# Layer 1's keys and queries by seven half-size products, in a hybrid attention kernel

## The chip, the cores and the metric

The kernel runs on one core of one Trainium2 chip. The metric is the device time of the whole program in microseconds; the runs of the kernel before took 3247.21, 3250.87 and 3253.22 us, and their median is 3250.87 us.

## The reference, cut to what matters

Four residual layers on `x` of shape (4, 1024, 256), all in fp32: attention "a", a feed-forward layer (256 to 1024 to 256, exact GELU), attention "b" (low-rank queries, keys and values with rotary tables), and the feed-forward layer again. Each works on a layer-normalised `x`. Layer 1 is attention "a", with 16 heads of 64:

```python
q = jnp.einsum('bsm,hmd->bhsd', x, kernel[0])
k = jnp.einsum('bsm,hmd->bhsd', x, kernel[1])
v = jnp.einsum('bsm,hmd->bhsd', x, kernel[2])
scale = jnp.float32(1.0 / (d * d * h))
scores = jnp.einsum('bhsd,bhtd->bhst', q, k) * scale
attn = jax.nn.softmax(scores, axis=-1)
out = jnp.einsum('bhst,bhtd->bhsd', attn, v)
```

The output is projected by `WO` and added to `x`. The widths are m = 256 and, for two heads together, 128 rows of q and of k for 1024 positions.

## The kernel before, in words

**Order.** All order on an engine is the order of the calls in the source (`manual_schedule`); a framework adds the semaphores and, where a tile is taken again, the wait for its last readers. Layer 1 has 4 batches times 8 pairs of heads = 32 pairs, numbered g. A pair has 8 steps, one for each 128 query rows (for both heads), so there are 256 steps.

**One step s** (`steps_with`, L339 to L371). It runs a software pipeline: `invert(s)` (reciprocal of the row sums on VectorE, L268, and its copy into the probabilities on ScalarE, L269); `scores(s + 1)` on TensorE (L247), eight matmuls into two PSUM tiles `sc`, one for each head; then for each head a row maximum on VectorE (L258) and an exponential on ScalarE (L260); `turn(s)`, a 32x32-block transpose of the probabilities on VectorE (L280); `send`, DMAs from SP and from GpSimd (L304) that put the blocks in place (`pT`); and, five steps later, for two steps at once, `weigh` (probabilities times values, L313), `take` (ScalarE copies L323, GpSimd product L325) and `project` (L176, ScalarE copy `got` L335, GpSimd add into `x` L337).

**Even and odd steps.** `weigh` and `take` run in odd steps, `project` in even ones. Two steps together, an even one and the odd one after it, are called a double step below; a pair has four of them.

**Preparing the next pair.** During the 8 steps of a pair the next pair's weights `w` are loaded by GpSimd's queue (L742) and its tiles are made, in the even steps. `qk` (L746 to L758) makes one half (512 positions) of kT or qT: four matmuls of 128x64x512 (two halves of the contraction, two heads side by side in the array), accumulated in one PSUM bank `mm`, and one ScalarE copy; it is called in all four even steps. `values` (L760 to L769) makes a quarter of v in each of four even steps. The work lists hold (time, function); a time with `- EARLY` (0.5) is issued between the step's two exponentials, a whole number at the step's end. Once per batch of 8 pairs the next batch's rows are normalised and transposed (`batch_a`, L156, L162, L165), in even steps.

**PSUM.** `ps_sc` has three buffers of two banks under the tag `sc`, `ps_mm` two of one bank (`m0`, `m1`, taken in turn by `group`). So scores take three buffers in rotation, and the new pair of tiles waits for the readers of the tiles taken three before.

**Tables.** `w1_sb`, `w2_sb`, the rotary tables and small ones are loaded at the start by GpSimd's queue (`load_rest`, L100).

Of the kernel before, what the change touches and what calls it, by code (L numbers as in the profile page):

```python
# [33 lines left out]
NK2 = S // DH  # L34
EPS = 1e-5
EARLY = 0.5
PLACES = {
# [11 lines left out]
def hybrid_block_kernel(  # L49
# [23 lines left out]
    pool = lambda name, bufs: ctx.enter_context(tc.tile_pool(name=name, bufs=bufs))  # L73
    pp, tp, ptp, otp, tmp = pool("p", 2), pool("T", 2), pool("pT", 2), pool("oT", 1), pool("tmp", 1)
    lowp, highp, xnp, rp = pool("low", 2), pool("high", 1), pool("xn", 1), pool("rope", 1)
    qkp, vp, wp, wop = pool("qk", 2), pool("v", 2), pool("wp", 2), pool("wo", 2)


# [12 lines left out]
    lnb_sb = const.tile([P, NC], F32, name="lnb_sb")  # L91

    w1_sb = const.tile([P, NC, F], F32, name="w1_sb")
    w2_sb = const.tile([P, NF, D], F32, name="w2_sb")
    b2_sb = const.tile([P, D], F32, name="b2_sb")
    wd_sb = const.tile([P, 2, NC, P], F32, name="wd_sb")
    cos_sb = const.tile([P, S], F32, name="cos_sb")
    sin_sb = const.tile([P, S], F32, name="sin_sb")

    def load_rest():  # L100
        for b in range(1, B):
            nc.sync.dma_start(xs[b], xv[b])
        nc.gpsimd.dma_start(w1_sb, w1.rearrange("(c p) f -> p c f", p=P))
        nc.gpsimd.dma_start(w2_sb, w2.rearrange("(c p) d -> p c d", p=P))
# [3 lines left out]
        for j in range(2):  # L108
            nc.gpsimd.dma_start(cos_sb[j * DH : (j + 1) * DH, :], rope_cos)
            nc.gpsimd.dma_start(sin_sb[j * DH : (j + 1) * DH, :], rope_sin)  # L110
        nc.gpsimd.dma_start(b1_sb, b1.rearrange("(c p) -> p c", p=P))
        nc.gpsimd.dma_start(lns_sb, ln_s.rearrange("(c p) -> p c", p=P))
        nc.gpsimd.dma_start(lnb_sb, ln_b.rearrange("(c p) -> p c", p=P))


    def scaling(name, blocks, again=False):
# [41 lines left out]
    def transposed(dst, src, c, affine=None):  # L158
# [5 lines left out]
        if affine is None:  # L164
            nc.scalar.copy(dst[:, c, :], trf)  # L165
        else:
# [23 lines left out]
    def attention(prep_batch, prep_pair, wo, loader, lead, kept):  # L190
# [148 lines left out]
        def steps_with(others):  # L339
            for k, f in others:  # L340
                pieces.setdefault(k, []).append(f)
            for s in range(-1, n + LAG + 1):
                h, part = divmod(s - LAG, HB)
                ahead = 0 <= s + 1 < n
                if 0 <= s < n:
                    invert(s)
                if ahead:
                    scores(s + 1)
                if part == 1 and 0 <= s // HB - 1 < n // HB:
                    send(s // HB - 1, nc.gpsimd, sent[len(sent) - POOL_DMA :])  # L350
# [44 lines left out]
    def ffn(rows, store):  # L395
# [31 lines left out]
        def weights():  # L427

            wc = ptp.tile([P, SENT], F32, tag="pT", name="wc")
            s1 = wc[:, : 4 * hf * P].rearrange("p (s f) -> p s f", s=4)  # L430
            s2 = wc[:, 4 * hf * P : 8 * hf * P].rearrange("p (s f d) -> p s f d", s=4, f=hf)
            m = hf * P
            parts["w1"] = (s1, w1_sb[:, 0, :m], w1_sb[:, 1, :m], w1_sb[:, 1, m:])
            lo, hi = w2_sb[:, :hf], w2_sb[:, hf:]
            parts["w2"] = (s2, lo[:, :, :P], hi[:, :, :P], hi[:, :, P:])
            v = nc.vector
            work = four([s1[:, i] for i in range(4)], w1_sb[:, 0, :m], w1_sb[:, 1, :m], w1_sb[:, 0, m:], w1_sb[:, 1, m:], [v] * 4)
            work += other([s2[:, i] for i in range(4)], lo[:, :, :P], lo[:, :, P:], hi[:, :, :P], hi[:, :, P:], [nc.gpsimd] * 4)
            for f in work:
                f()  # L440

# [112 lines left out]
        def down_seven(n, hook):  # L554
            b, qb = blocks[n]
            t4, b11, b21, b22 = parts["w2"]
            s, g = sums.pop(n), gT[n]
            a11, a12, a22 = g[:, :hf, :half], g[:, hf:, :half], g[:, hf:, half:]
            pairs = {
                1: (a11, b11), 2: (a12, b21), 3: (s[:, 3], b22), 4: (a22, t4[:, 3]),  # L560
                5: (s[:, 0], t4[:, 0]), 6: (s[:, 1], t4[:, 1]), 7: (s[:, 2], t4[:, 2]),
            }
            xb = xs[b][:, ts(qb, TQ), :]
            x11, x12, x21, x22 = xb[:, :2, :P], xb[:, :2, P:], xb[:, 2:, :P], xb[:, 2:, P:]
# [1 line left out]

            def product(bank, k, first):
                l, r = pairs[k]
                product_of(bank, lambda t, f: l[:, f, ts(t, P)], lambda f: r[:, f], first, hf)

            def after(bank, k):
                bank = bank[:, :, :P]
# [37 lines left out]
        def down(n, t):  # L610
# [2 lines left out]
                po[n] = group(2, D)  # L613
            for f in range(NF):
                nc.tensor.matmul(  # L615
                    po[n][:, t % 2, :], gT[n][:, f, ts(t, P)], w2_sb[:, f, :],
                    start=(f == 0), stop=(f == NF - 1),
                )
            if t % 2:
# [8 lines left out]
    def ffn_between(rows, store, n_steps, nxt=None, prologue=(), ramp=None):  # L628
# [10 lines left out]
        ends += [(n - 2, lambda: rows.finish[0]()), (n - 2, lambda: normed(0)), (n - 1, lambda: turned(0))]  # L639
        ends += [(n - 1 + (0, 0, 0, 1, 2, 2, 3, 3)[f], lambda f=f: up(0, f)) for f in range(NF)]  # L640
        ends += [(n, lambda: normed(1))]
        ends += [(n + 1, lambda m=m, t=t: rows.measure(m, t)) for m in range(2, 6) for t in range(TQ)]
        ends += [(n + 2, lambda: rows.finish[1]()), (n + 2, weights), (n + 3, lambda: turned(1))]
        ends += [(n + 3, lambda: row_sums(1)), (n + 4, lambda: down(0, 0))]

        def rest():
# [3 lines left out]
            for m in range(1, last + 1):  # L650
# [11 lines left out]
                if m == 1:  # L662
                    for i in range(2 * TQ):
                        when(2 + i, lambda i=i: rows.measure(6 + i // TQ, i % TQ))
                if nxt and m >= 2:
                    for t in range(TQ):
                        when(5 + t, lambda m=m, t=t: nxt.measure(m - 2, t))
# [36 lines left out]

    def layer_a():

        scale_a = 1.0 / (DH * DH * H)
        hTs = {}
        rows = Rows("a", (blocks[:1], blocks[1:2], blocks[2:]))

        def batch_a(b):
            work = []
            for qb in range(NQB):
# [12 lines left out]
                def turned(c, b=b, k=k, qb=qb):  # L726
                    if c == 0:
                        p, tag = ((lowp, "low"), (highp, f"high{b % 2}"))[qb]
                        hTs[b, qb] = p.tile([P, NC, QB], F32, tag=tag, name="hT")
                    transposed(hTs[b, qb], k["xn"], c)  # L730

                work += [(10 * qb + t, lambda t=t, f=straight: f(t)) for t in range(TQ)]
                work += [(10 * qb + 6 + 2 * c, lambda c=c, f=turned: f(c)) for c in range(NC)]
            return work

        def pair_a(b, pr):
            made = {}
# [8 lines left out]
            def qk(i, qb):  # L746
# [7 lines left out]
                dst = made[name][:, ts(qb, QB)]  # L754
                if i == 0:
                    nc.scalar.mul(dst, pq, scale_a)
                else:
                    nc.scalar.copy(dst, pq)  # L758

            def values(m):  # L760
                if m == 0:
# [2 lines left out]
                for t in range(4):  # L764
# [4 lines left out]
                nc.scalar.copy(made["v"][:, ts(m, 4), :], pv)  # L769
# [19 lines left out]


        first = loads + [lambda: measured(0)] + xn[:4] + [lambda: measured(1), ready] + xn[4:6] + pair[:1]
        first += xn[6:] + pair[1:3]
# [4 lines left out]
    def layer_b(rows):  # L797
# [45 lines left out]
        def pair_b(b, pr):  # L843
# [23 lines left out]
            def rotate(i, qb):  # L867

                straight, other = made[i, qb], turned.pop((i, qb))
                nc.gpsimd.tensor_mul(straight, straight, cos_sb[:, ts(qb, QB)])  # L870
                nc.gpsimd.tensor_mul(other, other, sin_sb[:, ts(qb, QB)])  # L871
                nc.gpsimd.tensor_add(straight, straight, other)

            def values(qb):
# [94 lines left out]
```

## Time and profile before

| | |
|---|---|
| runs of the kernel before | 3247.21, 3250.87, 3253.22 us; median 3250.87 |
| the profiled execution | 3250.15 us, of which the span of the trace is 3248.4 us |
| granted TensorE clock | 0.996 |
| busy in the span | TensorE 3164.4 us (97%), VectorE 2723.5 (84%), ScalarE 2137.9 (66%), GpSimd 2002.1 (62%) |
| layer 1 | from the start to about 1415 us; feed-forward to about 1690; layer 3 to about 3000; feed-forward to the end |

The profile shows one execution. A line such as `L260 ACT` is line 260 of the kernel on ScalarE; PE is TensorE's matmuls, PEld its weight loads (they run ahead of the matmuls), DVE is VectorE, POOL is GpSimd, SP issues DMAs. In a timeline the first two numbers are the start in us from the start of the span and the length; an arrow in brackets says how long the engine stood idle before and what ended that. A weight load that waits for a semaphore shows when a matmul was released.

### The profile page before, as it was taken

To read this page: it belongs to the slowest core of one execution; us is meant where nothing else is said; L and a number is where in the kernel's file an instruction comes from. 1 tells how busy PE (TensorE), PEld (TensorE's weight loads), DVE (VectorE), ACT (ScalarE), POOL (GpSimd) and SP (SyncE) were. 2 spreads that over 40 slices of the span, in tenths; PEclk is the share of its full clock that TensorE was granted. 3 is DMA by queue.
4 is the path that set the end of the run, shared out by engine and by line. 5 is a ranking of instruction groups with operands and counts; after the bars stand their busy time and mean duration, and the time that the engine had idled before them with its cause. 6 is when DMAs were issued, how large, how long until landed. Compare 5 with 4: busy or idle time off the path is not lost.

```text
span 3248.4 us, 128967 instructions
## 1 busy us (share of the span) xinstructions
PE 3164.4 (97%) x53648; PEld 2092.2 (64%) x53648; DVE 2723.5 (84%) x2686; ACT 2137.9 (66%) x4400; POOL 2002.1 (62%) x2782
## 2 busy tenths in 40 slices
PE   8999999999999999999999999999999999999999
PEld 4666666666666666668866566666666666655688
DVE  7988888888888888966569989998999999999554
ACT  5666666666666666655447777777778777777542
POOL 4544545455444545442249889899899889886311
PEclk9999999999999999999999999999999999999999
DMA  8888888888888888850029889988989899988200
GB/s 228 217 224 215 224 224 228 217 219 222 221 217 225 219 231 223 221 150 1 4 74 244 225 228 243 242 237 236 246 243 243 234 240 246 238 235 221 57 20 27
DMA packets 244709, 642.29 MB, mean 198 GB/s; under 512 B 74304, under 2 KB 102976, under 8 KB 244128
## 3 DMA queue, kind: packets, MB, share of 16 engines
q1 hardware_dynamic: 161104, 397.60, 48.0%
q0 software_dynamic: 83024, 236.44, 26.0%
q8 instruction: 426, 6.98, 1.0%
q14 instruction: 155, 1.27, 0.1%
HBM read 43.39 MB, written 4.19 MB: 15 GB/s over the span
## 4 chain that ended last, share of the span: by engine, by line
PE 69%; SPq 12%; DMA 6%; DVE 5%; ACT 4%; issue 3%; POOL 1%; DVEq 0%; ACTq 0%; POOLq 0%
PE sc L247 20%; PE mm L313 19%; PE mm L176 15%; SPq L304 11%; DMA pT<-T 5%; PE pw L495 4%; PE mm L185 4%; PE mm L495 3%; PE mm L615 2%; DVE T L280 2%; DVE nmax L258 1%; ACT p L260 1%; PE ph L604 1%; ACT gT L529 1%; PE mm L162 1%
## 5 line engine op out<-in xcount | busy, mean ns | idle before, releaser
L258 DVE TENSOR_REDUCE nmax<-sc 128x1 f32<-128x1024 f32 x1024 | 1204.5, 1218 | 214.3 <-PE sc L247 211.3
L260 ACT ACTIVATE p<-sc,nmax 128x1024 f32<-128x1024 f32 x1024 | 1145.3, 1119 | 322.3 <-DVE nmax L258 322.2
L280 DVE STREAM_TRANSPOSE T<-p 128x2176 f32<-128x2176 f32 x512 | 1247.3, 2436 | 48.4 <-DMA pT<-T 18.4
L247 PE MATMUL sc<-kT,qT 64*64 64x512 f32 x8192 | 1082.5, 598 | 11.9 <-ACT p L260 10.3
L313 PEld LDWEIGHTS mm<-pT,v 64*64 64x64 f32 x32768 | 949.5, 133 | 140.7 <-issue 98.5
L313 PE MATMUL mm<-pT,v 64*64 64x128 f32 x32768 | 983.0, 269 | 9.6 <-issue 8.5
L304 POOL DMA_DIRECT2D pT<-T x1280 | 629.6, 499 | 125.5 <-PE sc L247 57.7
L325 POOL TENSOR_TENSOR oT<-oT,pT 128x256 f32<-128x256 f32 x256 | 187.0, 730 | 696.3 <-ACT oT L323 623.0
L247 PEld LDWEIGHTS sc<-kT,qT 64*64 64x64 f32 x8192 | 332.8, 133 | 401.6 <-issue 274.5
L337 POOL TENSOR_TENSOR x<-x,got 128x512 f32<-128x512 f32 x256 | 331.0, 1293 | 25.8 <-ACT got L335 22.0
L335 ACT COPY got<-mm 128x512 f32<-128x512 f32 x256 | 150.0, 586 | 281.8 <-PE mm L176 281.8
L176 PE MATMUL mm<-wo,oT 128*64 128x256 f32 x2048 | 279.9, 394 | 24.1 <-POOL oT L325 22.8
L176 PEld LDWEIGHTS mm<-wo,oT 128*64 128x64 f32 x2048 | 124.9, 136 | 273.2 <-POOL oT L325 226.5
L269 ACT COPY p<-total 128x128 f32<-128x128 f32 x512 | 151.9, 297 | 198.6 <-DVE total L268 192.4
L176 PE MATMUL mm<-hT,w 128*64 128x512 f32 x1024 | 243.4, 597 | 0.9 <-ACT hT L165 0.9
L260 ACT ACTIVATION_READ_ACCUMULATOR p<-sc,nmax 128x1 f32 x1024 | 205.2, 200 | 0.0
L185 PEld LDWEIGHTS mm<-w,hT 128*64 128x64 f32 x4096 | 140.9, 138 | 71.3 <-issue 69.4
L871 POOL TENSOR_TENSOR turned<-turned,sin_sb 128x512 f32<-128x512 f32 x128 | 163.8, 1279 | 0.0
L409 POOL TENSOR_TENSOR x<-x,b_sb 128x256 f32<-128x256 f32 x64 | 48.8, 777 | 170.6 <-ACT xn L156 170.6
L296 ACT COPY pT<-T 32x1088 f32<-32x1088 f32 x128 | 140.3, 1096 | 4.9 <-DMA pT<-T 1.1
L185 PE MATMUL mm<-w,hT 128*64 128x64 f32 x4096 | 140.9, 222 | 0.2 <-ACT kT L758 0.2
L176 PEld LDWEIGHTS mm<-hT,w 128*64 128x64 f32 x1024 | 73.3, 138 | 96.8 <-issue 75.0
(145 smaller groups left out, 2928.5 us busy)
## 6 DMA issues: line engine op xcount, KB each, us to landing
pT<-T SPq DMA_DIRECT2D x2688, 136.0 KB, 4.7
pT<-T POOLq DMA_DIRECT2D x1280, 136.0 KB, 4.7
turned<-kT POOLq DMA_DIRECT2D x128, 128.0 KB, 3.4
turned<-qT POOLq DMA_DIRECT2D x128, 128.0 KB, 3.5
w<-in_wqkv_a POOLq DMA_DIRECT2D x96, 128.0 KB, 6.0
wo<-in_wo_a POOLq DMA_DIRECT2D x32, 128.0 KB, 5.4
wo<-in_wo_a POOLq DMA_DIRECT2D x64, 64.0 KB, 5.5
wo<-in_wo_b SPq DMA_DIRECT2D x32, 128.0 KB, 4.0
```

What stands on the lines that cost most here:

```text
L176: nc.tensor.matmul(out[ts(j, DH)], lhsT[:, ts(j, DH)], rhs[j], start=(first and i == 0), stop=(last and i == len(parts) - 1),)
L185: nc.tensor.matmul(out[ts(j, DH)], lhsT, rhs[:, ts(j, DH)], start=(i == 0), stop=(i == len(parts) - 1),)
L247: nc.tensor.matmul(sc[s, j][ts(half, DH), ts(m, 512)], qT()[rows, ts(2 * qs + half, DH)], kT()[rows, ts(m, 512)], start=True, stop=True,)
L258: nc.vector.tensor_reduce(nmax, sc[s, j], AX.X, ALU.max, negate=True)
L260: nc.scalar.activation(probs[s][:, :NK2, ts(j, 2), :], sc.pop((s, j)).rearrange("p (k c i) -> p k c i", c=2, i=SQ), AF.Exp, bias=nmax, acc ...
L280: nc.vector.transpose(T[h][:, :, q, :, :].rearrange("p c k i -> p k c i"), probs.pop(s))
L304: engine.dma_start(pT[h][ts(c, SQ), a], T[h][ts(a, SQ), c])
L313: nc.tensor.matmul(av[h][q][ts(j ^ q, DH)], v[ts(j, DH), k, :], pT[h][ts(j, DH), :, q, k, :], start=(k == 0), stop=(k == NK2 - 1),)
L325: nc.gpsimd.tensor_mul(parts, parts, pT.pop(h)[:, :, :, NK2, :])
L337: nc.gpsimd.tensor_add(xd, xd, got)
L495: nc.tensor.matmul(bank[:, t, : right(k).shape[-1]], left(t, k), right(k), start=(first and t == 0 and k == 0), stop=(k == n_k - 1), skip_ ...
L871: nc.gpsimd.tensor_mul(other, other, sin_sb[:, ts(qb, QB)])
```

## The change

Keys and queries together are the matrix [q; k] = W h with W of 2x2 blocks (q or k by half of the contraction) and h of 2x2 blocks (half of the contraction by half of the positions): eight block products. The change makes them, for all pairs but the first, by the Winograd form of Strassen's scheme: seven block products and sums of blocks.

- `row_sums`: four sums of blocks of hT for each batch, on VectorE, 128x512 each. They stand at times 21 to 24 of the batch's list, one per step (for the first batch in the prologue).
- `weight_sums`: four sums of 128x128 blocks of `w` for each pair, on GpSimd, two steps before the first product.
- `products`: products 1 and 6 in the first even step, 7 and 5 in the second, 4 and 2 in the third, 3 alone in the fourth. A product is two matmuls of 128x64x512. Two products of a step share one new tile `pw` of the score buffers (`ps_sc`, tag `sc`); product 3 takes a bank from `group` as before and is copied at once.
- `copied`: one ScalarE copy for each of the first three, at the new time `- MIDDLE` (0.25), which is after the step's second exponential; before, each copy stood between the two exponentials.
- `added`: at the step's end; one VectorE sum of PSUM with SBUF for each of the first three (128x512), and on GpSimd two sums after products 7 and 5, one after 4 and 2, one after 3.
- The scale is split: hT is scaled by its root on the copy out of the transposes, and v is scaled back on its copy.
- The tables: w2 and the rotary tables are not loaded at the start. Their space (pool `tail`) holds the sums; w2 is loaded by SP's queue in four pieces at steps 250 to 253, the rotary tables in the feed-forward layer. The feed-forward layer's sums of w2 are made in eight half-width GpSimd instructions in place of four.

```diff
+MIDDLE = 0.25
+    tail = pool("tail", 1)
-    w2_sb = const.tile([P, NF, D], F32, name="w2_sb")
-    cos_sb = const.tile([P, S], F32, name="cos_sb")
-    sin_sb = const.tile([P, S], F32, name="sin_sb")
...
+    def load_w2(i):
+        held["w2", i] = tail.tile([P, 2, D], F32, tag=f"w2{i}", name="w2_sb")
+        rows = w2.rearrange("(c p) d -> p c d", p=P)
+        nc.sync.dma_start(held["w2", i], rows[:, ts(i, 2), :])
...
                 if part == 0 and 0 <= h < n // HB:
                     take(h)
+                for f in pieces.get(s - MIDDLE, ()):
+                    f()
                 if 0 <= s < n:
                     turn(s)
...
+            if b:
+                work += [(21 + i, lambda i=i: row_sums(b, i)) for i in range(4)]
...
+        def row_sums(b, i):
+            if i == 0:
+                sums[b] = [tail.tile([P, 2, QB], F32, tag=t, name="hs") for t in ("cos", "sin")]
+            t = [sums[b][k // 2][:, k % 2] for k in range(4)]
+            h = [[hTs[b, qb][:, c, :] for qb in range(NQB)] for c in range(NC)]
+            left, right = ((h[0][1], h[0][0]), (h[1][1], t[0]), (h[1][1], h[0][1]), (h[1][0], t[1]))[i]
+            nc.vector.tensor_sub(t[i], left, right)
...
+            def weight_sums():
+                s = made["s"] = tail.tile([P, 4, P], F32, tag="w20", name="ws")
+                (q0, q1), (k0, k1) = [[made["w"][:, i, c, :] for c in range(NC)] for i in range(2)]
+                nc.gpsimd.tensor_add(s[:, 0], k0, k1)
+                nc.gpsimd.tensor_sub(s[:, 1], s[:, 0], q0)
+                nc.gpsimd.tensor_sub(s[:, 2], q0, k0)
+                nc.gpsimd.tensor_sub(s[:, 3], q1, s[:, 1])
+            def products(which):
+                w, s, t = made["w"], made["s"], [sums[b][k // 2][:, k % 2] for k in range(4)]
+                h = [[hTs[b, qb][:, c, :] for qb in range(NQB)] for c in range(NC)]
+                sides = {
+                    1: (w[:, 0, 0], h[0][0]), 2: (w[:, 0, 1], h[1][0]), 3: (s[:, 3], h[1][1]),
+                    4: (w[:, 1, 1], t[3]), 5: (s[:, 0], t[0]), 6: (s[:, 1], t[1]), 7: (s[:, 2], t[2]),
+                }
+                if which == (3,):
+                    made[3] = group(QB)
+                else:
+                    both = ps_sc.tile([P, 2, QB], F32, tag="sc", name="pw")
+                    for i, k in enumerate(which):
+                        made[k] = both[:, i]
+                for k in which:
+                    l, r = sides[k]
+                    paired(made[k], [(l, [r] * 2)])
+                if which == (3,):
+                    nc.scalar.copy(made["qT"][:, QB:], made[3])
+            def copied(which):
+                if which == (1, 6):
+                    made["x1"] = tail.tile([P, QB], F32, tag="w21", name="x1")
+                    nc.scalar.copy(made["x1"], made[1])
+                elif which == (7, 5):
+                    made["kT"] = qkp.tile([P, S], F32, tag="kT", name="kT")
+                    nc.scalar.copy(made["kT"][:, QB:], made[5])
+                elif which == (4, 2):
+                    made["qT"] = qkp.tile([P, S], F32, tag="qT", name="qT")
+                    nc.scalar.copy(made["qT"][:, :QB], made[2])
+            def added(which):
+                q, k = made.get("qT"), made.get("kT")
+                if which == (1, 6):
+                    made["u2"] = tail.tile([P, QB], F32, tag="w22", name="u2")
+                    nc.vector.tensor_add(made["u2"], made[6], made["x1"])
+                elif which == (7, 5):
+                    made["u3"] = tail.tile([P, QB], F32, tag="w23", name="u3")
+                    nc.vector.tensor_add(made["u3"], made[7], made["u2"])
+                    nc.gpsimd.tensor_add(made["u2"], made["u2"], k[:, QB:])
+                    nc.gpsimd.tensor_add(k[:, QB:], k[:, QB:], made["u3"])
+                elif which == (4, 2):
+                    nc.vector.tensor_add(k[:, :QB], made[4], made["u3"])
+                    nc.gpsimd.tensor_add(q[:, :QB], q[:, :QB], made["x1"])
+                else:
+                    nc.gpsimd.tensor_add(q[:, QB:], q[:, QB:], made["u2"])
...
-            work = [(4 - 4 * i + 2 * qb - EARLY, lambda i=i, qb=qb: qk(i, qb)) for i in (1, 0) for qb in range(NQB)]
+            if b == 0 and pr == 0:
+                work = [(0, lambda i=i, qb=qb: qk(i, qb)) for i in (1, 0) for qb in range(NQB)]
+            else:
+                work = [(-2, weight_sums)]
+                for i, which in enumerate(((1, 6), (7, 5), (4, 2), (3,))):
+                    work += [(2 * i - EARLY, lambda which=which: products(which))]
+                    work += [(2 * i - MIDDLE, lambda which=which: copied(which))]
+                    work += [(2 * i, lambda which=which: added(which))]
```

More of the change, by code (lines that the diff above doesn't have):

```diff
@@ L93, in hybrid_block_kernel @@
     w1_sb = const.tile([P, NC, F], F32, name="w1_sb")
-    w2_sb = const.tile([P, NF, D], F32, name="w2_sb")
     b2_sb = const.tile([P, D], F32, name="b2_sb")
     wd_sb = const.tile([P, 2, NC, P], F32, name="wd_sb")
-    cos_sb = const.tile([P, S], F32, name="cos_sb")
-    sin_sb = const.tile([P, S], F32, name="sin_sb")
+    held = {}
     def load_rest():
@@ L103, in load_rest @@
         nc.gpsimd.dma_start(w1_sb, w1.rearrange("(c p) f -> p c f", p=P))
-        nc.gpsimd.dma_start(w2_sb, w2.rearrange("(c p) d -> p c d", p=P))
         nc.gpsimd.dma_start(b2_sb, b2.partition_broadcast(P))
@@ L107, in load_rest @@
             nc.gpsimd.dma_start(wd_sb[:, i], w.rearrange("(c p) r -> p c r", p=P))
-        for j in range(2):
-            nc.gpsimd.dma_start(cos_sb[j * DH : (j + 1) * DH, :], rope_cos)
-            nc.gpsimd.dma_start(sin_sb[j * DH : (j + 1) * DH, :], rope_sin)
         nc.gpsimd.dma_start(b1_sb, b1.rearrange("(c p) -> p c", p=P))
@@ L113, in load_rest, with w2_of, load_rope @@
         nc.gpsimd.dma_start(lnb_sb, ln_b.rearrange("(c p) -> p c", p=P))
+    def load_w2(i):
+        held["w2", i] = tail.tile([P, 2, D], F32, tag=f"w2{i}", name="w2_sb")
+        rows = w2.rearrange("(c p) d -> p c d", p=P)
+        nc.sync.dma_start(held["w2", i], rows[:, ts(i, 2), :])
+    def w2_of(f):
+        return held["w2", f // 2][:, f % 2, :]
+    def load_rope():
+        for name, table in (("cos", rope_cos), ("sin", rope_sin)):
+            held[name] = tail.tile([P, S], F32, tag=name, name=name)
+            for j in range(2):
+                nc.sync.dma_start(held[name][j * DH : (j + 1) * DH, :], table)
     def scaling(name, blocks, again=False):
@@ L156, in standardize, with transposed @@
         nc.scalar.activation(dst, src, AF.Identity, scale=rstd, bias=shift)
-    def transposed(dst, src, c, affine=None):
+    def transposed(dst, src, c, affine=None, scale=None):
         tr = group(TQ, P)
@@ L163, in transposed @@
         trf = tr.rearrange("p t q -> p (t q)")
-        if affine is None:
+        if affine is None and scale is None:
             nc.scalar.copy(dst[:, c, :], trf)
+        elif affine is None:
+            nc.scalar.mul(dst[:, c, :], trf, scale)
         else:
@@ L433, in weights @@
             parts["w1"] = (s1, w1_sb[:, 0, :m], w1_sb[:, 1, :m], w1_sb[:, 1, m:])
[L434 to L438, printed above, removed]
+            parts["w2"] = (
+                s2, lambda f: w2_of(f)[:, :P], lambda f: w2_of(hf + f)[:, :P], lambda f: w2_of(hf + f)[:, P:]
+            )
+            work = four([s1[:, i] for i in range(4)], w1_sb[:, 0, :m], w1_sb[:, 1, :m], w1_sb[:, 0, m:], w1_sb[:, 1, m:], [nc.vector] * 4)
+            for h in range(2):
+                lo, hi = held["w2", h], held["w2", 2 + h]
+                work += other(
+                    [s2[:, i, ts(h, 2)] for i in range(4)],
+                    lo[:, :, :P], lo[:, :, P:], hi[:, :, :P], hi[:, :, P:], [nc.gpsimd] * 4,
+                )
             for f in work:
@@ L556, in down_seven @@
             t4, b11, b21, b22 = parts["w2"]
+            t1, t2, t3, t4 = [lambda f, i=i, t=t4: t[:, i, f] for i in range(4)]
             s, g = sums.pop(n), gT[n]
@@ L559, in down_seven @@
             pairs = {
-                1: (a11, b11), 2: (a12, b21), 3: (s[:, 3], b22), 4: (a22, t4[:, 3]),
-                5: (s[:, 0], t4[:, 0]), 6: (s[:, 1], t4[:, 1]), 7: (s[:, 2], t4[:, 2]),
+                1: (a11, b11), 2: (a12, b21), 3: (s[:, 3], b22), 4: (a22, t4),
+                5: (s[:, 0], t1), 6: (s[:, 1], t2), 7: (s[:, 2], t3),
             }
@@ L568, in product @@
                 l, r = pairs[k]
-                product_of(bank, lambda t, f: l[:, f, ts(t, P)], lambda f: r[:, f], first, hf)
+                product_of(bank, lambda t, f: l[:, f, ts(t, P)], r, first, hf)
             def after(bank, k):
@@ L615, in down @@
                 nc.tensor.matmul(
-                    po[n][:, t % 2, :], gT[n][:, f, ts(t, P)], w2_sb[:, f, :],
+                    po[n][:, t % 2, :], gT[n][:, f, ts(t, P)], w2_of(f),
                     start=(f == 0), stop=(f == NF - 1),
@@ L641, in ffn_between @@
         ends += [(n, lambda: normed(1))]
+        if nxt:
+            ends += [(n - 6 + i, lambda i=i: load_w2(i)) for i in range(4)]
         ends += [(n + 1, lambda m=m, t=t: rows.measure(m, t)) for m in range(2, 6) for t in range(TQ)]
@@ L664, in rest @@
                         when(2 + i, lambda i=i: rows.measure(6 + i // TQ, i % TQ))
+                    if nxt:
+                        when(20, load_rope)
                 if nxt and m >= 2:
@@ L705, in layer_a @@
     def layer_a():
-        scale_a = 1.0 / (DH * DH * H)
+        root = 1.0 / DH / H**0.5
+        sums = {}
         hTs = {}
@@ L729, in turned @@
                         hTs[b, qb] = p.tile([P, NC, QB], F32, tag=tag, name="hT")
-                    transposed(hTs[b, qb], k["xn"], c)
+                    transposed(hTs[b, qb], k["xn"], c, scale=root)
                 work += [(10 * qb + t, lambda t=t, f=straight: f(t)) for t in range(TQ)]
                 work += [(10 * qb + 6 + 2 * c, lambda c=c, f=turned: f(c)) for c in range(NC)]
-            return work
+            if b:
+                work += [(21 + i, lambda i=i: row_sums(b, i)) for i in range(4)]
+            return work
+        def row_sums(b, i):
[5 more added lines that the diff above has]
+            nc.vector.tensor_sub(t[i], left, right)
         def pair_a(b, pr):
@@ L753, in qk @@
                 ])
-                dst = made[name][:, ts(qb, QB)]
-                if i == 0:
-                    nc.scalar.mul(dst, pq, scale_a)
-                else:
-                    nc.scalar.copy(dst, pq)
+                nc.scalar.copy(made[name][:, ts(qb, QB)], pq)
+            def weight_sums():
[5 more added lines that the diff above has]
+                nc.gpsimd.tensor_sub(s[:, 3], q1, s[:, 1])
@@ L768, in values @@
                     ])
-                nc.scalar.copy(made["v"][:, ts(m, 4), :], pv)
-            work = [(4 - 4 * i + 2 * qb - EARLY, lambda i=i, qb=qb: qk(i, qb)) for i in (1, 0) for qb in range(NQB)]
+                nc.scalar.mul(made["v"][:, ts(m, 4), :], pv, 1.0 / root)
+            if b == 0 and pr == 0:
[6 more added lines that the diff above has]
+                    work += [(2 * i, lambda which=which: added(which))]
             work += [(6 + 2 * m, lambda m=m: values(m)) for m in range(NT // 2)]
@@ L791, in layer_a @@
         first = loads + [lambda: measured(0)] + xn[:4] + [lambda: measured(1), ready] + xn[4:6] + pair[:1]
-        first += xn[6:] + pair[1:3]
+        first += xn[6:] + pair[1:3] + [lambda i=i: row_sums(0, i) for i in range(4)]
         later += [((-1, 0, 0, 1, 1)[i], f) for i, f in enumerate(pair[3:])]
@@ L869, in rotate @@
                 straight, other = made[i, qb], turned.pop((i, qb))
-                nc.gpsimd.tensor_mul(straight, straight, cos_sb[:, ts(qb, QB)])
-                nc.gpsimd.tensor_mul(other, other, sin_sb[:, ts(qb, QB)])
+                nc.gpsimd.tensor_mul(straight, straight, held["cos"][:, ts(qb, QB)])
+                nc.gpsimd.tensor_mul(other, other, held["sin"][:, ts(qb, QB)])
                 nc.gpsimd.tensor_add(straight, straight, other)
```

## The prediction

> **What bounds the kernel now.** First the busy times of a stretch deep in layer 1, then the chain of waits there, in order of time (start, us, what).
>
> ```profile
> 600.00:800.00 200.00, 199.52 (x3792) 124.80 (x3792) 172.57 (x146) 129.09 (x282) 97.67 (x153) 1.00 0.85 218
> ```
>
> ```profile
> 617.04 1.72 PE sc L247 x16
> 618.76 2.73 PE mm L176 x16
> 621.49 0.93 PE mm L185 x32
> 622.42 1.88 PE sc L247 x16
> 624.29 3.49 PE mm L313 x128
> ```
>
> TensorE is busy 199.5 of 200 us, VectorE 172.6; the chain is TensorE alone. One double step is 1.72 + 2.73 + 0.93 + 1.88 + 3.49 = 10.75 us; four are a pair, 43.0 us. The 2.73 is `project` and one `qk`; in the timeline `qk` is 619.60 to 621.32, 1.72 us for four matmuls, 0.43 each. Less TensorE work shortens the kernel as long as nothing else comes up. So next: what else is near. The timeline of an even step:
>
> ```profile
> 619.87 0.59 ACT L335 COPY got<-mm 128x512 f32<-128x512 f32 x1 [1.19 <-PE mm L176]
> 620.36 1.12 ACT L260 ACTIVATE p<-sc,nmax 128x1024 f32<-128x1024 f32 x1
> 621.53 0.60 ACT L756 ACTIVATE qT<-mm 128x512 f32<-128x512 f32 x1
> 622.03 1.11 ACT L260 ACTIVATE p<-sc,nmax 128x1024 f32<-128x1024 f32 x1
> 622.35 1.95 PE L247 MATMUL sc<-kT,qT 64*64 64x512 f32 x16
> 623.12 0.37 ACT L769 COPY v<-mm 128x256 f32<-128x256 f32 x1
> ```
>
> The next scores start at 622.35, while the second exponential (622.03) still runs: with three buffers they need only the first one's. And VectorE:
>
> ```profile
> 618.81 2.35 DVE L258 TENSOR_REDUCE nmax<-sc 128x1 f32<-128x1024 f32 x2 [0.46 <-PE sc L247]
> 621.08 2.43 DVE L280 STREAM_TRANSPOSE T<-p 128x2176 f32<-128x2176 f32 x1
> 623.44 0.12 DVE L268 RECIPROCAL total<-total 128x2 f32<-128x2 f32 x1
> 624.35 2.36 DVE L258 TENSOR_REDUCE nmax<-sc 128x1 f32<-128x1024 f32 x2 [0.78 <-PE sc L247]
> ```
>
> It idles 0.46 and 0.78 us for scores: work of 9.5 in 10.75. Last, the end of layer 1, where no pair is prepared any more and TensorE has 1.72 us less to do per double step: the change's effect in the trace of before.
>
> ```profile
> 1381.64 0.63 PEld L176 LDWEIGHTS mm<-wo,oT 128*64 128x64 f32 x8 [0.81 <-POOL oT L325]
> 1383.31 1.12 ACT L260 ACTIVATE p<-sc,nmax 128x1024 f32<-128x1024 f32 x1
> 1384.32 0.20 ACT L260 ACTIVATION_READ_ACCUMULATOR p<-sc,nmax 128x1 f32 x1
> 1384.41 1.12 ACT L260 ACTIVATE p<-sc,nmax 128x1024 f32<-128x1024 f32 x1
> 1384.57 0.21 PEld L247 LDWEIGHTS sc<-kT,qT 64*64 64x64 f32 x8 [0.80 <-ACT p L260]
> 1391.65 0.63 PEld L176 LDWEIGHTS mm<-wo,oT 128*64 128x64 f32 x8 [0.81 <-POOL oT L325]
> ```
>
> Here a double step takes 10.01 us, not 10.75 - 1.72 = 9.03. The scores' weights wait for the first exponential: its accumulator read ends at 1384.52, the load follows at 1384.57, 1.26 us after that exponential began. A loop is seen: release to project 7.08 (1384.57 to 1391.65), project to `got` 1.19, to the exponential 0.48, to release 1.26; sum 10.01.
>
> **The change, part by part.**
>
> *Product tile in the score buffers (the main term).* In three of a pair's four even steps a tile `pw` is taken between two pairs of score tiles. Counting in threes, the scores after it then need the buffers of both score tiles before it, so they wait for the second exponential too; the semaphores in the changed program's instruction order say the same (first score matmul on the first exponential, second on the second). The second begins 1.10 us after the first (1383.31, 1384.41), so the loop becomes 10.01 + 1.10 = 11.11, against 10.75 of TensorE work, which these steps keep (two products are four matmuls, as `qk`): +0.36 us. Ends: 0.16, if the release came without the 0.20 read; 0.58, if exponential and read lay end to end (1.12 + 0.20). I take 0.36, as the tail shows both pieces. Behind the waiting score matmul in TensorE's queue stand `weigh`, the next scores and `project`; nothing there can go first. That the copies move behind the exponentials is in this number: where `qk`'s copy stayed between them (0.50, from 621.53 to 622.03), each step would cost 0.5 more.
>
> *Fourth even step.* One product of 0.86 us goes. The scores wait only for the first exponential here, 10.01; the copy of product 3 still stands between the exponentials, so v's copy ends 3.13 us after the first one's start (620.36 to 623.49), and `weigh` takes that bank. Its main part would start at 1.26 + 1.77 (622.35 to 624.12) = 3.03; with 0.05 of release it waits 0.15. So 10.16: -0.59 (ends: -0.86; -0.31, if the 0.28 waits for v's copy seen before came in full).
>
> *Count.* Of 31 pairs the first falls in the ramp. The other 30 have 90 product steps; 9 of these hold a transpose of the next batch (0.58 of TensorE work after `values`), where 11.33 already covers 11.11. So 81 x 0.36 = 29.2; 30 x 0.59 = 17.7, and three fourth steps with transposes get nearer to 0.86, together 18.5.
>
> *Ramp.* At 39.80, 44.45, 49.10 VectorE's maxima follow each other at 4.65 us, set by VectorE. With the longer release a round is 1.24 (maximum to exponential, 39.80 to 41.04) + 1.13 + 1.26 + 2.00 (load to maximum, 622.35 to 624.35) = 5.63; three times +0.98: 2.9.
>
> *VectorE's sums.* The feed-forward layer's 128x512 sum of PSUM and SBUF (L535) takes 0.69. One per product step makes 9.5 + 0.7 = 10.2 of 11.1: hidden by the 0.78 gap, which stays; uncovered it would cost 0.69. `row_sums` put four more into two double steps of a batch; the fourth step then has 9.5 + 1.4 = 10.9 of work for 10.16, about 0.8 late, three batches: 2.4.
>
> *GpSimd's sums.* 1.29 for 128x512 (L337), 0.73 for 128x256 (L325); for 128x128 I estimate 0.45 by that slope. Queued behind them are `take`'s product and the `pT` sends. Worst are the two after products 7 and 5: VectorE's sum ends about 624.2, they end 626.8; `take`'s copies ended 628.31. Weight sums: `x` sum to 622.7, one sum to 624.0, four to 625.8, `wo` issues 1.6 to 627.4, against 627.7. Price 0, 0.4 per pair if they were late.
>
> A sum may be slower beside GpSimd: in the seam after layer 1 a `wc` sum took 1.10 (L421) against 0.68 (L423), GpSimd's L325 1.21 against 0.73. The Trainium skill (SBUF — State Buffer, Who interferes with whom) says why: a VectorE instruction with two SBUF inputs and a GpSimd one that reads SBUF exclude each other, one with a PSUM input does not. By it only the 12 `row_sums` are exposed, an estimate of under 12 x 0.5 us; without it all 105 sums would be.
>
> *The rest.* ScalarE has as many copies as before, with v's as a scaled one. Fewer loads at the start gain nothing: TensorE there waits for hT's and kT's copies. w2's four loads stand in SP's queue among sends with five steps of lead, the rotary loads in a stage with 0.00 DMA share. `weights` on GpSimd: eight of 0.73 for four of 1.27, +0.8, ending 1448.6 where its next waits until 1448.62. Together 0.
>
> **Sum.** 29.2 - 18.5 + 2.9 + 2.4 = +16.0. On the profiled execution, 3250.15 us (0.72 below the median of 3250.87): 3266 us.
>
> **The rivals.**
> *A, the wait is not met: faster.* If releases come such that scores after a product start when TensorE is ready, the 29.2 and the 2.9 go: 3250.15 - 18.5 + 2.4 = 3234; with 0.86 in full 3227. It decides where the second exponential's release is 0.36 us earlier. For: TensorE is the whole chain now. Against: the 0.80 wait of the tail, for the earlier of the two. 0.11.
> *B, a draw.* At 0.20 per product step the 81 cost 16.2 and the sum is +3.0: 3253. For: the first score matmul needs only the first exponential and can go ahead. Against: in the tail it does (1383.58) and the load-to-project time stays 7.08, as elsewhere (611.60 to 618.68). 0.09.
> *C, GpSimd late.* `take`'s product behind the sums makes `project` late, 0.4 us in two double steps of each pair: 30 x 0.8 = 24, 3290. For: TensorE's loads for `project` wait for it already. Against: the 0.3 to 1.5 us of cover above. 0.12.
> That the work isn't cut is out: matmuls for q and k go from 16 to 14 a pair in the instruction order.
>
> **How the numbers follow.** 0.2%, 6.5 us, is about what a measurement can tell from no change. Forecast 0.68, C 0.12: slower 0.80; B 0.09; A 0.11. All low ends give 81 x 0.16 - 25.8 = -12.8, 3237; all high ends 81 x 0.58 - 9.3 + 5.3 = +43, 3293. Leaving A and the outer half of C out: 3252 to 3283.
>
> **What would show it.** Right: in the chain, pairs of three double steps of 11.1 and one of 10.2; score loads waiting for ACT L260 some 80 times; fewer busy us of TensorE over a longer layer 1; unchanged layers after. Wrong: product steps of 10.75 with no such wait (A), or `project` waiting for POOL L325 by more than now (C).

## The result

The changed kernel takes 3269.78 us in the median of five runs (3260.89 to 3270.34), the kernel before 3250.87 (3247.21 to 3259.49); the ratio is 1.0049, with a 95% interval from 1.0029 to 1.0069. By the ratio that is 16 us more. It is slower, though TensorE has an eighth less to do for keys and queries. The two profiled spans are 3266.1 and 3248.4 us, 17.7 apart.

The busy times of the same stretch as before, deep in layer 1 (PE, PEld, DVE, ACT, POOL; then the clock, the DMA share and GB/s):

```profile
600.00:800.00 200.00, 197.41 (x3692) 129.72 (x3687) 179.86 (x162) 124.94 (x272) 125.46 (x184) 0.99 0.82 215
```

TensorE now idles 2.6 us of 200, where it idled 0.5, and GpSimd is busy for 125.5 us, where it was 97.7. The chain of waits there, in order of time:

```profile
610.55 1.72 PE sc L261 x16
612.27 1.01 PE mm L190 x8
613.28 1.72 PE pw L190 x8
615.00 0.93 PE mm L199 x32
615.93 1.97 PE sc L261 x14
617.89 3.44 PE mm L327 x118
621.66 1.72 PE sc L261 x15
```

In these rows it is still TensorE alone by name; from 629.33 the chain goes over VectorE, SP's queue and a transfer to GpSimd and comes back to TensorE only at 646.66, in the late step that run 6 is about. (The trace has two records for each matmul call: the two products of a step, four calls, are x8.) But the scores at 615.93 and `weigh` behind them reach to 621.66, 5.73 us, where they took 1.88 + 3.49 = 5.37 before: 0.36 more for the same instructions, with the other pieces of the step as long as they were. The timeline of this product step shows why:

```profile
612.19 0.63 PEld L190 LDWEIGHTS mm<-wo,oT 128*64 128x64 f32 x8 [0.81 <-POOL oT L339]
613.38 0.59 ACT L349 COPY got<-mm 128x512 f32<-128x512 f32 x1 [1.19 <-PE mm L190]
613.86 1.12 ACT L274 ACTIVATE p<-sc,nmax 128x1024 f32<-128x1024 f32 x1
614.96 1.11 ACT L274 ACTIVATE p<-sc,nmax 128x1024 f32<-128x1024 f32 x1
615.86 0.19 PEld L261 LDWEIGHTS sc<-kT,qT 64*64 64x64 f32 x2
615.96 0.21 ACT L274 ACTIVATION_READ_ACCUMULATOR p<-sc,nmax 128x1 f32 x1
616.22 0.25 PEld L261 LDWEIGHTS sc<-kT,qT 64*64 64x64 f32 x7 [0.18 <-ACT p L274]
616.95 0.65 DVE L845 TENSOR_TENSOR u<-pw,u 128x512 f32<-128x512 f32 x1
623.30 0.63 PEld L190 LDWEIGHTS mm<-wo,oT 128*64 128x64 f32 x8 [0.81 <-POOL oT L339]
```

The next scores load two weights at 615.86, for the tile that the first exponential has freed, and then stand until 616.22: the second exponential's accumulator read ends at 616.17, 0.05 earlier. From one projection to the next are 623.30 - 612.19 = 11.11 us. The bracket says only 0.18, since it counts from the end of the two loads that went ahead (616.05); the loss is read from the distance of the projections. VectorE's sum, 0.65 at 616.95, comes after all this. Over 100 to 1400 us the view of waits has:

```profile
PEld mm L190 <- POOL oT L339: 100.2, 115, 3.0
DVE nmax L272 <- PE sc L261: 93.1, 165, 1.9
POOL oT L339 <- DMA pT<-T: 48.0, 19, 6.4
PEld sc L261 <- ACT p L274: 17.4, 82, 1.0
```

The score loads wait for an exponential 82 times (3 times before). VectorE, which has the sums to do, waits less for scores (136.3 us before). `take`'s product on GpSimd waits for a transfer 19 times (3 before), and the longest wait of `project`'s loads is now 3.0 us (1.2 before); runs 6 to 10 go after these two.

To see the whole layer, the distances between projections were taken from the trace, 115 of them from the fifth on, and sorted by kind. "Transpose" is a double step that also transposes the next batch.

| double steps | number | before, sum | after, sum | difference | median before, after |
|---|---|---|---|---|---|
| product steps | 77 | 834.3 | 864.8 | +30.5 | 10.75, 11.11 |
| product steps with a transpose | 9 | 102.0 | 104.6 | +2.6 | 11.34, 11.34 |
| fourth steps | 26 | 282.6 | 273.4 | -9.2 | 10.75, 10.15 |
| fourth steps with a transpose | 3 | 37.3 | 33.2 | -4.1 | 12.54, 11.08 |
| all | 115 | 1256.3 | 1276.1 | +19.8 | |

Outside that stretch the two profiles differ by +0.6 at the start, -0.6 at the layer's end, -4.2 in the feed-forward layer after it, and +2.0 in layer 3. Layer 3 took 1332.5 to 1343.6 us in the ten profiles of kernels that leave GpSimd's queue five transfers per double step or give it four (runs 7 and 8 give it six), so +2.0 is no more than one execution differs from another.

### The profile page after: what moved, and what is told of

Its sections match the earlier page's. It is cut to its first block, busy times and chain, and to the rows that moved or that the text cites. A ratio compares the mean times of both kernels' runs of the same rounds, so it can differ in the third digit from the quotient of the medians.

```text
span 3266.1 us, 129208 instructions
## 1 busy us (share of the span) xinstructions
PE 3173.8 (97%) x53524; PEld 2139.4 (66%) x53524; DVE 2787.4 (85%) x2795; ACT 2129.6 (65%) x4400; POOL 2209.0 (68%) x3033
## 4 chain that ended last, share of the span: by engine, by line
PE 64%; SPq 15%; DMA 6%; DVE 5%; ACT 4%; issue 3%; POOL 1%; DVEq 0%; ACTq 0%; POOLq 0%
PE sc L261 19%; PE mm L327 17%; SPq L318 14%; PE mm L190 9%; DMA pT<-T 5%; PE pw L190 5%; PE pw L516 4%; PE mm L199 4%; PE mm L516 3%; PE mm L637 2%; DVE T L294 2%; DVE nmax L272 2%; ACT p L274 1%; PE ph L626 1%; POOL oT L339 1%
## 5 line engine op out<-in xcount | busy, mean ns | idle before, releaser
L261 PE MATMUL sc<-kT,qT 64*64 64x512 f32 x8192 | 1147.0, 597 | 17.5 <-ACT p L274 14.3
L327 PEld LDWEIGHTS mm<-pT,v 64*64 64x64 f32 x32768 | 985.0, 133 | 113.9 <-issue 101.7
L327 PE MATMUL mm<-pT,v 64*64 64x128 f32 x32768 | 1016.3, 269 | 7.6 <-issue 6.1
L261 PEld LDWEIGHTS sc<-kT,qT 64*64 64x64 f32 x8192 | 385.1, 132 | 406.7 <-issue 247.2
L972 POOL TENSOR_TENSOR turned<-turned,sin 128x512 f32<-128x512 f32 x128 | 163.8, 1280 | 0.0
L190 PE MATMUL mm<-hc,w 128*64 128x512 f32 x512 | 133.5, 599 | 0.0
L337 ACT COPY oT<-mm 128x128 f32<-128x128 f32 x512 | 110.0, 267 | 11.9 <-PE mm L327 11.3
```

Of the source, the lines that this page charges most:

```text
L190: nc.tensor.matmul(out[ts(j, DH)], lhsT[:, ts(j, DH)], rhs[j], start=(first and i == 0), stop=(last and i == len(parts) - 1),)
L261: nc.tensor.matmul(sc[s, j][ts(half, DH), ts(m, 512)], qT()[rows, ts(2 * qs + half, DH)], kT()[rows, ts(m, 512)], start=True, stop=True,)
L327: nc.tensor.matmul(av[h][q][ts(j ^ q, DH)], v[ts(j, DH), k, :], pT[h][ts(j, DH), :, q, k, :], start=(k == 0), stop=(k == NK2 - 1),)
L972: nc.gpsimd.tensor_mul(other, other, held["sin"][:, ts(qb, QB)])
```

## The experiments

Theory W: a product's tile in the three score buffers makes the next scores wait for the second exponential, and that wait alone makes a product step 11.11. Rival S: the added sums, on VectorE or GpSimd, set it. Rival T, taken up in run 5: the tables loaded late carry part of the loss. Ratios are to the kernel before, run on the same chip. Its median lay between 3250.87 and 3258.44 from one set of runs to the next, so ratios are compared and not times.

**1. The copy back between the exponentials.**

```diff
-work += [(2 * i - MIDDLE, lambda which=which: copied(which))]
+work += [(2 * i - EARLY, lambda which=which: copied(which))]
```

> The changed kernel, with ScalarE's copy of a product put back between a step's two exponentials; everything else as it is. Theory W (the next scores wait for the second exponential, and that is what makes a product step 11.11 us): the copy waits for the products (they end 1.05 us after the first exponential begins) and takes 0.59, so the second exponential starts about 0.5 us later and the product steps go from 11.11 to 11.6; 81 of them by 0.5 and 9 with transposes by 0.3 make +43: 3313 us beside 3270, 1.019 of the kernel before. Rival S (the added sums on VectorE and GpSimd set 11.11): the sums start where they did or 0.5 earlier, no change, 3265 to 3275.

Measured: 3315.59 us, ratio 1.0177 (1.0162 to 1.0192). The median product step is 11.67, a fourth step still 10.15; the 77 product steps are 39 us longer than in the changed kernel. Its timeline:

```profile
910.31 1.12 ACT L274 ACTIVATE p<-sc,nmax 128x1024 f32<-128x1024 f32 x1
911.49 0.59 ACT L831 COPY kT<-pw 128x512 f32<-128x512 f32 x1
911.97 1.12 ACT L274 ACTIVATE p<-sc,nmax 128x1024 f32<-128x1024 f32 x1
913.23 0.21 PEld L261 LDWEIGHTS sc<-kT,qT 64*64 64x64 f32 x8 [0.74 <-ACT p L274]
```

The second exponential begins 1.66 us after the first, not 1.10, and the step is 0.56 longer: the second exponential sets it, one for one. From its start to the load that it frees are 913.23 - 911.97 = 1.26 us, as in the other kernel. W holds; S, which foresaw no change, does not.

**2. The wait alone, in the kernel before.**

```diff
-pq = group(QB)
+pq = ps_sc.tile([P, 2, QB], F32, tag="sc", name="pw")[:, 0]
...
+work += [(4 - 4 * i + 2 * qb - MIDDLE, lambda i=i, qb=qb: copied(i, qb))]
```

> The kernel before, with the bank of each of its four q and k products taken from the score buffers, and its copy moved behind the second exponential; no Strassen, no sums, no late tables. Theory W: all four double steps of a pair go from 10.75 to 11.11, 30 pairs, less the 12 steps that a transpose already makes longer: 108 x 0.36 = 39, 3290 us, 1.012. Rival S: without sums nothing is late, 3251, 1.000.

Measured: 3293.89 us, ratio 1.0112 (1.0097 to 1.0127), +36 by the ratio. All four double steps have a median of 11.11 us. No sum was added and no product was cut:

```profile
814.77 0.63 PEld L177 LDWEIGHTS mm<-wo,oT 128*64 128x64 f32 x8 [0.81 <-POOL oT L326]
816.44 1.12 ACT L261 ACTIVATE p<-sc,nmax 128x1024 f32<-128x1024 f32 x1
817.54 1.11 ACT L261 ACTIVATE p<-sc,nmax 128x1024 f32<-128x1024 f32 x1
818.80 0.25 PEld L248 LDWEIGHTS sc<-kT,qT 64*64 64x64 f32 x7 [0.18 <-ACT p L261]
```

The same release, 1.26 us after the second exponential's start. So the buffer rotation, with the copy behind the second exponential as in the change, is enough for the whole 0.36.

**3. The sums taken away.** GpSimd's sums and the row sums on VectorE are left out of the changed kernel.

```diff
-work = [(-2, weight_sums)]
+work = []
...
-nc.gpsimd.tensor_add(made["u2"], made["u2"], k[:, QB:])
-nc.gpsimd.tensor_add(k[:, QB:], k[:, QB:], made["u3"])
...
```

> The changed kernel without GpSimd's sums (the four of a pair's weights, the four 512-wide ones behind the products) and without VectorE's sums of the activations; raw blocks stand as operands, so that part of the computation is left out, while every product, copy and VectorE sum behind a product stays. Theory W: product steps stay 11.11 and the fourth 10.15; the row sums (2.4) and the two fourth steps where GpSimd was late (4) go: 3260 to 3267, 1.003 to 1.005. Rival S: the 0.36 of the 81 product steps goes, 29 less, 3241, 0.997.

Measured: 3277.67 us, ratio 1.0064 (1.0047 to 1.0081), not told apart from the changed kernel's 1.0049. The medians stay 11.11 and 10.15. In the 115 double steps of the profile 4.3 us are saved, 1271.8 against 1276.1; the total doesn't show them, and the 3260 to 3267 us that W gave did not come. VectorE's sums behind the products stay in this run, but run 2 has none of them and its steps take 11.11 all the same. So rival S is out by the two runs together.

**4. The projection's copy behind the exponentials.** If W holds, whatever lets the second exponential start earlier shortens the step.

```diff
-                    project(h)
+                    add = project(h)
...
+                if part == 1 and 0 <= h < n // HB and late:
+                    add()
```

`add` is the copy `got` and GpSimd's sum into `x`; the second place is behind both exponentials.

> The changed kernel; in product steps without a transpose ScalarE's copy of the projection (got) and GpSimd's add to x stand behind both exponentials instead of ahead of the first. Theory W: the first exponential no longer waits for got and starts 0.3 us earlier, the second then follows the second maximum, 0.21 earlier; so the product steps go from 11.11 to 10.91, 81 x 0.2 = 16 less: 3254, 1.001. Rival S: the sums are as they were, no change, 3265 to 3275, 1.005.

Measured: 3257.61 us, ratio 1.0011 (1.0002 to 1.0020): 12 us less than the changed kernel by the ratios. The median product step falls to 10.85 in two of the three, where 10.91 was expected; the one right after a fourth step is at 11.02. The 77 product steps are 18.4 us shorter.

```profile
784.37 0.63 PEld L190 LDWEIGHTS mm<-wo,oT 128*64 128x64 f32 x8 [0.81 <-POOL oT L340]
784.49 2.36 DVE L273 TENSOR_REDUCE nmax<-sc 128x1 f32<-128x1024 f32 x2 [0.46 <-PE sc L262]
785.75 1.11 ACT L275 ACTIVATE p<-sc,nmax 128x1024 f32<-128x1024 f32 x1 [1.39 <-DVE nmax L273]
786.88 1.11 ACT L275 ACTIVATE p<-sc,nmax 128x1024 f32<-128x1024 f32 x1
787.89 0.19 ACT L275 ACTIVATION_READ_ACCUMULATOR p<-sc,nmax 128x1 f32 x1
787.98 0.57 ACT L352 COPY got<-mm 128x512 f32<-128x512 f32 x1
788.03 0.30 PEld L262 LDWEIGHTS sc<-kT,qT 64*64 64x64 f32 x8
```

The first exponential now waits for VectorE's maximum alone (1.39). The second begins 2.51 us after the projection's load, where it was 2.77, and 0.26 is by how much the step is shorter. The 0.10 that is left above 10.75 is still the second exponential: its accumulator read ends at 788.08. Of the eight loads in the row at 788.03 the first two, for the tile that the first exponential freed, begin at once; the other six begin from 788.13 on, 0.05 after that read, so that the row lasts 0.30 us and not the 0.21 of eight that go on together. They are 0.10 late, and so are `weigh` behind them and the next projection, at 795.21 (10.84 after this one). The fourth steps gave some back (277.7 us for 26, against 273.4, with a median of 10.50); why is not shown.

**5. The tables alone.** The kernel before with w2 and the rotary tables loaded late.

```diff
-nc.gpsimd.dma_start(w2_sb, w2.rearrange("(c p) d -> p c d", p=P))
+ends += [(n - 6 + i, lambda i=i: load_w2(i)) for i in range(4)]
...
+    when(20, load_rope)
```

> The kernel before with only the late tables of the change: w2 in four loads on SP near the end of layer 1, the rotary tables in the feed-forward stage, w2's sums in eight GpSimd instructions; no Strassen in the pairs. Theory W, in which the product steps make the whole difference: the layers and the seam as before, ratio 1.000, within 4 us of the kernel before. Rival T (the tables carry part of the 16 to 19 us): at least 1.002, or below 0.998 if the earlier start seen in the changed kernel's trace (1.0 us) and its shorter seam (4.2 us) are the tables' doing; then the product steps cost some 4 us more than the total shows.

Measured: 3251.02 us, ratio 0.9987 (0.9976 to 0.9999). That is within 0.2% of no change, so the tables carry none of the loss; by the ratio they give back some 4 us, by the far end of its interval 8, and the product steps would then cost that much more than the total shows. Its feed-forward layer took 254.4 us from projection to projection, against 256.2 before and 252.0 after; of other kernels, run 2 with the instructions of the kernel before there gave 252.0, run 3 with those of the changed kernel 256.6. So the -4.2 seen between the two profiles is within the spread of single executions.

**6. The weight sums behind `take`.**

```diff
-work = [(-2, weight_sums)]
+work = [(-1, weight_sums)]
```

> The changed kernel, with GpSimd's four sums of a pair's weights one step later, behind take's product instead of ahead of it. Theory W with rival C in part (GpSimd is late in a few fourth steps only): the product steps stay 11.11, the two fourth steps of 12.25 and the step after one of them (13.03) come down, 4 to 6 us less: 3265, 1.003 of the kernel before. If C held in every pair (0.4 us in two double steps), 20 us less: 3250, 0.999. If GpSimd is never what project waits for: no change, 1.005.

The reason for it is in the changed kernel's timeline, one of its two fourth steps of 12.25 and 12.28 us:

```profile
634.41 0.63 PEld L190 LDWEIGHTS mm<-wo,oT 128*64 128x64 f32 x8 [0.81 <-POOL oT L339]
639.01 0.97 POOL L318 DMA_DIRECT2D pT<-T  x2 [2.74 <-issue]
641.24 1.29 POOL L852 TENSOR_TENSOR qT<-qT,u 128x512 f32<-128x512 f32 x1
643.84 0.45 POOL L801 TENSOR_TENSOR ws<-w,ws 128x128 f32<-128x128 f32 x1
645.87 0.74 POOL L339 TENSOR_TENSOR oT<-oT,pT 128x256 f32<-128x256 f32 x1
646.66 0.41 PEld L190 LDWEIGHTS mm<-wo,oT 128*64 128x64 f32 x6 [2.92 <-POOL oT L339]
```

GpSimd's queue stood still for 2.74 us without a releaser in the profile (the last section says how often that comes), and behind it came the sum of q, four weight sums and the loads of `wo`, so `project` waited 2.92. Measured: 3270.23 us, ratio 1.0054 (1.0037 to 1.0071). The two steps come down to 10.48 and 10.46, the 13.03 behind one of them to 11.34, and the 115 double steps take 1273.0 us, 3.1 less; but the whole does not differ from the changed kernel's 1.0049, where 1.003 was expected. C held in two of 29 pairs, not in every pair.

**7 to 10. Which queue sends the blocks.** A transposed tile goes out in 16 blocks of 136 KB, eleven from SP and five from GpSimd. These runs move one, in layer 1 only; runs 9 and 10 have a minus where the first line shows the plus of runs 7 and 8.

```diff
+by_pool = POOL_DMA + (kept == 0)
...
-send(s // HB, nc.sync, sent[: len(sent) - POOL_DMA])
+send(s // HB, nc.sync, sent[: len(sent) - by_pool])
```

Run 7, on top of runs 4 and 6:

> The kernel with got behind both exponentials, and two more edits: the weight sums one step later as in the run above, and six of the sixteen blocks of a transposed tile sent from GpSimd's queue in layer 1 instead of five. Theory D (with product steps at 10.85, the rest of the loss is VectorE's transpose waiting for the blocks that SP sends last): the steps after a fourth step go from 11.1 to 10.85 in the median and the sum over steps of what exceeds 10.85 and 10.15 falls from 33 to under 20: 0.996 of the kernel before, 3243. Rival (that excess is the memory system's own and goes wherever blocks are sent from): 1.000, 3256.

Run 8, on the kernel before:

> The kernel before with six blocks instead of five sent from GpSimd's queue in layer 1, nothing else. Theory D: TensorE's 10.75 stays, what exceeds it in some steps (20 us over the layer, 12 of 116 steps holding a transpose account for 7) loses up to 6: 0.998 to 1.000. Rival: the sixth block makes take's product late in each double step (0.5 us each, 60 us): 1.018.

Measured: 3291.58 us, ratio 1.0112 (1.0092 to 1.0132), and 3279.19, 1.0074 (1.0053 to 1.0094). Theory D falls: the sixth block from GpSimd makes both kernels slower, and neither the gain of D nor the 0.5 us in each double step of its rival is seen. In run 8's profile the 115 double steps take 10.9 us more and layer 3, whose instructions are the same, 17.7 more.

Run 9, on the kernel before, and run 10, on run 4's:

> The kernel before with four blocks instead of five sent from GpSimd's queue in layer 1, twelve from SP's. With six the layer lost 11 us, and layer 2, whose instructions are the same, 18. Theory G (blocks from GpSimd's queue cost more than from SP's, which still idles 2.4 us per double step): 0.997 to 1.000. Theory D (SP's last blocks are what VectorE's transpose waits for; a twelfth takes 0.78 us of the 2.4): 1.002 to 1.006.

> The kernel with got behind both exponentials, and four blocks instead of five sent from GpSimd's queue in layer 1. Theory G: less than 1.001, down to 0.997, with product steps of 10.85 and fewer steps above it. Theory D: 1.004 or more, since here SP has least room behind the short fourth steps (1.6 us).

Measured: run 9 3246.94 us, ratio 0.9964 (0.9950 to 0.9978); run 10 3248.14 us, 0.9970 (0.9957 to 0.9982). Both beat both kernels, and not each other. With four blocks Strassen's products, with the projection's copy late, are worth nothing more than the old `qk`. The gain is not located: run 9's 115 double steps took 1256.4 us, as before (1256.3), in a profiled execution of 3250.10 us, above that kernel's median.

## Why the prediction was right, point by point

**The main term.** A product step of 11.11 was foretold from the tail of the trace before, as a loop of 10.01 with the 1.10 between two exponentials, and 11.11 was measured; run 2 got it from the rotation alone, and runs 1 and 4 moved it by what they moved the second exponential (+0.56, -0.26). In sum the 77 product steps of the stretch cost 30.5 us, where 77 x 0.36 is 27.7; the 2.8 above it lie in single late steps. Run 1 also bears out the 0.5 for a copy left between the exponentials (0.56). The nine with a transpose were taken at 11.33 and free; seven were, two were late (13.03 and 12.14).

**The fourth step.** Predicted 10.16, measured 10.15, for the reason given:

```profile
149.00 0.63 PEld L190 LDWEIGHTS mm<-wo,oT 128*64 128x64 f32 x8 [0.81 <-POOL oT L339]
151.91 0.23 PEld L261 LDWEIGHTS sc<-kT,qT 64*64 64x64 f32 x8
153.34 0.40 ACT L863 ACTIVATE v<-mm 128x256 f32<-128x256 f32 x1
159.14 0.63 PEld L190 LDWEIGHTS mm<-wo,oT 128*64 128x64 f32 x8 [0.81 <-POOL oT L339]
```

From the scores' loads to the next projection are 7.23 us, where the tail had 7.08. The 0.15 is `weigh` waiting for v's copy, which ends at 153.74; its loads for that bank begin at 153.79. In sum this term was too large: 26 x 0.59 = 15.3 us of gain were counted and 9.2 came. Late steps take up the rest: the two of 12.25 and 12.28 (4.2 us together), which the term did not hold, and the three with row sums (11.05, 11.08 and 10.51; 2.2 us together, priced apart at 2.4). That price is right in size only: run 3 has no row sums, and the same three steps take 11.49, 10.92 and 10.14 there, 2.1 us together. The three transposed fourth steps gave 4.1 us where 3 x 0.86 = 2.6 was taken, but they end at 11.08, not at the 10.5 that this would make of 11.33. The transposes wait there for product 3's copy, whose bank they need (L174 for ACT L822, up to 0.6 us, in the view of waits), which the prediction did not look for; that they gained more is because three of before's took 12.22 to 12.55.

**Ramp and ends.** Here the step from one round to three failed: +2.9 was taken, +0.6 came. The round that was looked at did go from 4.65 to 5.60 (maxima at 38.36 and 43.96). But the other two had been 6.07 and 5.18 long before (29.06 to 35.13, 49.10 to 54.28), not 4.65, and became 5.63 and 5.78. So the maxima fell 1.1 us behind over the rounds, and everything began 1.0 us earlier. That start isn't steady: the first projection stands at 59.05 us in the kernel before and from 59.2 to 63.3 in the others. The loads left out at the start were priced at nothing; run 5 leaves them some 4 us of gain at its ratio, and doesn't show where it would lie.

**Sums.** VectorE's sums take 0.65, estimated 0.69, and are hidden; GpSimd's 128x128 ones 0.45, as estimated. The trace has rows now for the rule of the Trainium skill (SBUF — State Buffer, Who interferes with whom) that the prediction leaned on:

```profile
627.83 1.28 POOL L850 TENSOR_TENSOR qT<-qT,x 128x512 f32<-128x512 f32 x1 [0.54 <-ACT qT L834]
628.05 0.65 DVE L849 TENSOR_TENSOR kT<-pw,u 128x512 f32<-128x512 f32 x1
...
687.44 0.47 POOL L798 TENSOR_TENSOR ws<-w 128x128 f32<-128x128 f32 x1
687.53 0.94 DVE L772 TENSOR_TENSOR hs<-hT,hs 128x512 f32<-128x512 f32 x1
687.98 0.79 POOL L799 TENSOR_TENSOR ws<-ws,w 128x128 f32<-128x128 f32 x1
...
693.07 0.65 DVE L772 TENSOR_TENSOR hs<-hT 128x512 f32<-128x512 f32 x1
```

A VectorE sum with one input in PSUM is 0.65 us beside a GpSimd sum as without it. A row sum, with both inputs in SBUF, is 0.94 beside GpSimd's sums and 0.65 with next to nothing beside it, and the GpSimd sum beside it 0.79 for 0.47. This agrees with the rule, and of the change's VectorE sums the row sums are the only exposed ones; 12 of them are too few to show in the total.

**The total.** +16.0 was predicted, +16 is the ratio's, but parts of it offset each other: in the stretch the same terms give 27.7 - 15.3 - 2.6 + 2.4 = +12.2 and +19.8 was measured; the ramp is 2.3 below its price, the feed-forward layer 4.2 shorter, and what is left is within what one execution differs from another. So the main term is understood, but that the total came out to the microsecond is luck.

**The rivals.** A would have needed product steps of 10.75 without a wait; 82 waits are there. B needed 0.20 per product step; the median took 0.36. C's mechanism is real in two pairs of 29, 3.1 us of the profiled time by run 6, and not told apart in the total.

## What to carry to other kernels

When a change takes work from the bounding engine and puts its result into buffers that another loop rotates through, count the rotation: which reader must now be done before that loop's next tile. Its price is the distance from the old releaser to the new one, less the slack of the loop, and a stretch of the old trace in which the bounding engine is less loaded shows that slack. Then pull the new releaser forward: moving one copy that does not feed it took back 12 of the 16 us. What the cut in TensorE's work would bring with the products outside that rotation was not measured.

## What the runs showed of the hardware

Which queue issues a transfer mattered about as much as the change did. Moving one of sixteen 136 KB blocks in layer 1 from SP's queue to GpSimd's gave 1.0074, moving one the other way 0.9964. The median time from issue to landing is 4.6 to 4.9 us in either queue (kernel before, runs 8 and 9), so it doesn't show the cause. The Trainium skill (DMA: Bandwidth & Descriptors, SWDGE vs HWDGE vs iDMA) says that GpSimd's transfers have their descriptors computed by software on it and that the other kind is set up faster, which agrees in sign; that this is the cause is not shown. Why layer 3, with the same instructions and the same five blocks, took 17.7 us longer in run 8's profile than in that of the kernel before, and 21.2 longer in run 7's than in the changed kernel's, stays open, as does where run 9 gains.

GpSimd's queue pauses without a releaser in the profile: six times between 100 and 1400 us in the changed kernel, for 2.72 to 3.03 us, 16.8 us together. This is not at random. Counted in the trace, 121 DMA issues of GpSimd lie between one such pause and the next, and in all twelve profiles the pauses of over 2 us are 121 issues or a multiple of 121 apart. In time that is 199 to 212 us here, 175 to 177 in run 8, where GpSimd sends six blocks, and 237 to 244 in run 9, where it sends four. What the queue does there the profile doesn't say. Whether a pause costs anything depends on what is queued behind it.

An exponential that also gives a row sum frees what waits for it only after the separate read of its accumulator: 1.26 us after its start in the kernel before (1383.31 to 1384.57), the changed one (614.96 to 616.22), run 1 (911.97 to 913.23) and run 2 (817.54 to 818.80), of which the exponential itself is 1.1.
